# A state-space stage: two tiles per operand, waited for by rotation or by region

## The chip, the cores and the metric

The kernel runs on one core of one Trainium2 chip. The metric is the device time of one execution in microseconds (us). The engines are TensorE (PE, matmuls into the PSUM banks; PEld is its weight loading), VectorE (DVE), ScalarE (ACT), GpSimd (POOL) and SyncE (SP, whose queue issues most of the DMAs). Each engine works through its own instructions in order; between engines, an instruction waits on semaphores.

## The reference

The whole program is a state-space block of two layers with a fusing batch norm, then a sparse quadratic convolution, then two rounds of a Fourier mixing layer and a quantized feed-forward layer, on a batch of 4 images of 96 channels and 64 x 64 points. Only the state-space block matters here. For each of two layers, with 4096 positions, 192 inner channels and 16 states:

```python
h = (seq - mu) * jax.lax.rsqrt(var + EPS) * ln_g + ln_b
xz = h @ in_w
xs, z = jnp.split(xz, 2, axis=-1)
xp = jnp.pad(xs, ((0, 0), (DCONV - 1, 0), (0, 0)))
xc = sum((conv_w[:, k] * xp[:, k:k + L, :] for k in range(DCONV))) + conv_b
xc = jax.nn.silu(xc)
dbl = xc @ xproj_w
...
delta = jax.nn.softplus(dt @ dt_w + dt_b)
dA = jnp.exp(delta[..., None] * A)
dBx = delta[..., None] * Bm[:, :, None, :] * xc[..., None]
hstates = jax.lax.associative_scan(comb, (dA, dBx), axis=1)[1]
y = jnp.einsum('blds,bls->bld', hstates, Cm) + Dp * xc
y = y * jax.nn.silu(z)
return y @ out_w
```

`xc` is the convolution's result and `z` the gate's input of the change's name. In the kernel they are the tiles `xcv` and `zs`.

## The kernel before

The state-space stage is `_mamba`. Its work is cut into 32 **units** (L161 to L164): a unit is one chunk of 512 positions, one layer and one pair of batch images. The 192 inner channels of two images are 384 rows, kept as three parts (k = 0, 1, 2) of 128 partitions: the first 128 channels of each image, and the last 64 of both. `xcv` and `zs` are therefore tiles of 128 x 3 x 512.

A unit has two halves of work. The **front** (`front`, with `norm` before it) makes its operands: six matmul groups `mm_i` (j = 0 to 5, L256 to L267), j = 0 to 2 for the convolution's three parts, with four taps each, j = 3 to 5 for the gate's three parts. ScalarE copies each out of PSUM, into `xcv[:, j, :]` (L275) or `zs[:, k, :]` (L277), then applies SiLU to each whole tile in place (L279, L280). Then come the projection `mm_dbl` from `xcv`, the step sizes `dl`, their product with `xcv` on GpSimd (`du`, L339), and the layouts that are written to DRAM. The **steps** are 24 per unit (three parts, four rows of eight channels, two halves): a DMA broadcasts the step sizes into an `a` tile (L434, eight buffers), ScalarE makes the decays from it (L452), TensorE broadcasts the inputs into a `pq` tile in PSUM (L447, three buffers of two banks), VectorE multiplies it (L457) and scans twice (L469), GpSimd multiplies the scanned states (L475), TensorE sums them into `py` (L488). Every eighth step ends a part: `gate` (L492) on VectorE makes y from `xcv[:, k, :]` and `py` (L496), and GpSimd multiplies it by `zs[:, k, :]` (L497). In a step with `apart` true, GpSimd multiplies a DMA broadcast `db` instead of VectorE a `pq`.

Every `mm_...` tile shares **one** PSUM buffer (tag "mm", one bank), so each matmul group waits until ScalarE or VectorE has read the group before.

The order is written out by hand (`manual_schedule`, L535 on). While the steps of unit n run, the front of unit n+1 is made: generators hand out one piece in each step's `side.slot()`. Within step s the order of issue is: broadcasts of s+2, the sum of an earlier pair of steps, one slot of side work, decays of s+3, the scans of s, the DMAs of later steps, the state copies, and in every eighth step a gate. The gate of part k=0 of a unit is issued in its step 10, that of k=1 in its step 18, that of k=2 in step 2 of the next unit. In that same step 2, in the slot ahead of the gate, the front of the unit after that makes its first write to `xcv`. Two units (the third and the last of the 32) are `late`: their front is issued from step 3 on, behind the output projection of the unit that they need.

`tail` (L359) holds the output projection `mm_o` of the unit before; `norm` normalizes the sequence through `mm_xc`, `mm_v` and `mm_r`, and VectorE writes `hn` from `mm_r` (L249).

The tiles of the change come from `tl(..., bufs=2)`: a rotation of two buffers under one tag. A new tile takes the buffer of the tile two units back, and its first write waits until every instruction that used the old tile is done.

After the stage, `_back` starts with its loads at L699 and uses the same memory; it works on the other layers.

Of the kernel before, what the change touches and what calls it, by code (L numbers as in the profile page):

```python
# [9 lines left out]
F32 = mybir.dt.float32  # L10
# [17 lines left out]
TC = 512  # L28
# [20 lines left out]
def _mamba(ctx, tc, io, w, fd, fstats, xsums):  # L49
# [11 lines left out]
    work = ctx.enter_context(tc.tile_pool(name="mwork", bufs=1))  # L61
# [93 lines left out]
    def col(l, n, k):  # L155

        at = l * 6 + n * 2 + (k == 2)
        return pv[:, at : at + 1]


    units = []  # L161
# [10 lines left out]
    def tag(unit):  # L172
        return "_".join(map(str, unit))

    def mm(nm, unit, shape=None):
        return ps_mm.tile(shape or [128, TC], F32, name=f"mm_{nm}{tag(unit)}", tag="mm")

    def tl(nm, unit, shape, dtype=F32, bufs=1, to=None):
        return work.tile(shape, dtype, name=f"{nm}_{tag(unit)}", tag=to or nm, bufs=bufs)

    def load(unit):
        ch, l, pr = unit
        if l == 0:
            for b in (2 * pr, 2 * pr + 1):
                xt = work.tile([C, TC], F32, name=f"x_{b}_{ch}", tag=f"x{b}")
                nc.sync.dma_start(xt, io["x"][b, :, ch * TC : (ch + 1) * TC])
                seq[b, ch, 0] = xt

    def norm(unit):

        ch, l, pr = unit
        bs = (2 * pr, 2 * pr + 1)
        xc, sqs, ps = {}, {}, {}

        def centred(n):
            xc[n] = tl(f"xc{n}", unit, [C, TC])
            nc.scalar.copy(xc[n], ps[n])
            sqs[n] = tl(f"sq{n}", unit, [C, TC])
            nc.scalar.activation(sqs[n], xc[n], AF.Square)

        for n, b in enumerate(bs):
            ps[n] = mm(f"xc{n}", unit, [C, TC])
            nc.tensor.matmul(ps[n], ctr, seq[b, ch, l], start=True, stop=True)
            if l == 0:
                nc.scalar.activation(
                    tl("xs", unit, [C, TC], to=f"sq{n}"), seq[b, ch, 0], AF.Identity, accum_out=xsums[:, b, ch : ch + 1]
                )
            yield
            centred(n)
            yield "free" if n == 0 else "gap"  # L210
        p_v = mm("v", unit, [128, 8])
        for n in range(2):
            for j in range(4):
                nc.tensor.matmul(
                    p_v[:, n * 4 + j : n * 4 + j + 1], sqs[n][:, j * 128 : (j + 1) * 128], mean1, start=True, stop=True
                )
        yield
        ve = tl("ve", unit, [128, 8])
        r = tl("r", unit, [128, 8])
        vh = tl("vh", unit, [128, 8])  # L220
        a = tl("ra", unit, [128, 8])
        nc.scalar.activation(ve, p_v, AF.Identity, bias=w["eps"])
        nc.scalar.activation(vh, ve, AF.Copy, scale=-0.5)
        yield "gap"
        nc.scalar.activation(r.bitcast(I32), ve.bitcast(I32), AF.Identity, bias=magic, scale=-0.5)
        for _ in range(3):
            nc.gpsimd.tensor_tensor(a, r, r, ALU.mult)
            nc.gpsimd.tensor_tensor(a, a, vh, ALU.mult)
            nc.gpsimd.tensor_scalar(a, a, 1.5, None, ALU.add)
            nc.gpsimd.tensor_tensor(r, r, a, ALU.mult)  # L230
        if ch:
            for b in bs:
                hn = hn_buf[b, l]
                nc.scalar.copy(hn[:, 0:3], hn[:, TC:])
        yield "gap"
        yield "gap"
        for n, b in enumerate(bs):
            p = mm(f"r{n}", unit, [C, TC])
            for j in range(4):
                nc.tensor.matmul(  # L240
                    p[:, j * 128 : (j + 1) * 128],
                    r[:, n * 4 + j : n * 4 + j + 1].to_broadcast([128, C]),
                    ident,
                    start=True,
                    stop=True,
                )
            yield
            yield
            nc.vector.tensor_tensor(hn_buf[b, l][:C, 3:], p, xc[n], ALU.mult)  # L249
            yield "free"  # L250

    def front(unit):
# [3 lines left out]
        for j in range(6):  # L256
            k = j % 3
            p = mm(f"i{j}", unit)
            taps = [(wk[l][:, t, :], t) for t in range(4)] if j < 3 else [(wz[l], 3)]
            for t, (wt, off) in enumerate(taps):  # L260
                cols = slice(off, off + TC)
                f = dict(start=t == 0, stop=t + 1 == len(taps))
                if k < 2:
                    nc.tensor.matmul(p, wt[:, 0:128], hn_buf[bs[k], l][:, cols], **f)  # L264
                else:
                    for n in range(2):
                        nc.tensor.matmul(p[64 * n : 64 * n + 64], wt[:, 128:DIN], hn_buf[bs[n], l][:, cols], **f)  # L267
                if t != 0 and t != 2 or len(taps) == 1:
                    yield
            if j == 0:  # L270
                xcv = tl("xcv", unit, [128, 3, TC], bufs=2)
            if j == 3:
                zs = tl("zs", unit, [128, 3, TC], bufs=2)
            if j < 3:
                nc.scalar.activation(xcv[:, j, :], p, AF.Identity, bias=col(l, 0, k))  # L275
            else:
                nc.scalar.copy(zs[:, k, :], p)  # L277
            yield "free"
# [51 lines left out]
        for at in range(6):  # L330
# [9 lines left out]
            if at >= 3:  # L340

                x, y, t = (t.bitcast(F32) for t in cut[at - 3])
# [192 lines left out]
    with tc.manual_schedule():  # L535
        for n in (0, 1):
            load(units[n])
        side.front = [weights(0), norm(units[0]), front(units[0])]
        side.drain()
        for s in range(5):  # L540
# [7 lines left out]
        for s in range(n_steps + NS):  # L548
# [5 lines left out]
            if at == 0:  # L554
                if n + 1 < len(units) and n + 1 not in late:
                    side.front += ([norm(units[n + 1])] if n == 0 else []) + [front(units[n + 1])]
                    side.norm += [weights(1)] * (n == 0)
            if at == 22 and n + 1 == len(units):
                side.tail.append(way_out(units[n]))
            if at == 3 and 0 < n < len(units):  # L560
                if n + 1 in late:
                    side.front = [tail(units[n - 1]), norm(units[n + 1]), front(units[n + 1])]
                else:
                    side.tail.append(tail(units[n - 1]))
# [5 lines left out]
            if s + 2 < n_steps:  # L570
                unit, k, r, h = steps[s + 2]
# [16 lines left out]
            while live and copied[0] < min(s + 8, n_steps):  # L588
                unit, k, r, h = steps[copied[0]]
# [813 lines left out]
@with_exitstack  # L1403
def kernel(ctx: ExitStack, tc: tile.TileContext, io, out):
    nc = tc.nc
    cp = ctx.enter_context(tc.tile_pool(name="common", bufs=1))
    dp = ctx.enter_context(tc.tile_pool(name="scratch", bufs=1, space=DRAM))
    w = _shared(nc, cp, io)
    p2 = [[dp.tile([2 * C, TC], F32, name=f"p2_{b}_{n}", tag=f"p2_{b}_{n}") for n in range(NCH)] for b in range(B)]
    fd = [dp.tile([C, L], F32, name=f"fd_{b}", tag=f"fd_{b}") for b in range(B)]  # L1410
    with tc.tile_pool(name="stats", bufs=1) as fp:
        fstats = fp.tile([C, B, NCH, 6], F32, name="fstats", tag="fstats")
        xsums = fp.tile([C, B, NCH], F32, name="xsums", tag="xsums")
        with ExitStack() as c:
            _mamba(c, tc, io, w, fd, fstats, xsums)
        with ExitStack() as c:
            _back(c, tc, io, w, fd, fstats, xsums, p2, out)
# [143 lines left out]
```

## Time and profile before

| | |
|---|---|
| median of 3 runs | 5200.37 us (5200.36 to 5221.51) |
| the profiled execution's own time | 5205.16 us |
| its span, first to last instruction | 5203.4 us |
| mean granted TensorE clock | 0.812 |
| busy: PE, DVE, ACT, POOL | 4082.1, 4317.2, 2680.5, 2849.5 us |
| first DMA of `_back` | 3054.44 us |
| DVE busy from 336 to 2861 us | 2331.18 us of 2525 |
| ACT, POOL, PE busy there | 1565.14, 2121.29, 1939.78 us |
| granted clock there | 0.75 |
| DMA share there | 0.85 |

The page gives busy time of each engine over the whole span and in 40 equal slices, each digit the busy share in tenths; a 9 is 90% or more. The row PEclk gives the TensorE clock that was granted, in tenths of full speed. The waits are counted where an engine was idle, and put to the instruction that ended last of those waited for. In an instruction's line of the timeline, "x4" counts the instructions merged into it, and the bracket holds the idle time of its engine just before and what ended it. The stretch from 336 to 2861 us runs from the k=2 gate (L496) of one unit to that of the unit 28 later; these units have a mean period of 90.2 us.

### The profile page before, as it was taken

The numbers are of one execution on the slowest core, as the hardware profiler recorded it, in microseconds if no ns is written. First come the engines' busy times: TensorE is split into PE (matmuls) and PEld (weight loads), VectorE is DVE, ScalarE is ACT, GpSimd is POOL, SyncE is SP. The second block draws the span as 40 slices with busy tenths as digits, with TensorE's granted clock in tenths as the row PEclk, the third lists the DMA queues.
The fourth block names the chain that finished last, engine by engine and source line by source line (L and its number), as shares of the span: only waits on it lengthen the run. The fifth ranks groups of instructions, "written<-read, shape, count | busy, mean of one in ns | idle before, by whom it ended". The sixth has DMA issues, their size and how long they took to land. (4 is left out here: it accounts for less than half of the span.)

```text
span 5203.4 us, 52872 instructions
## 1 busy us (share of the span) xinstructions
PE 4082.1 (78%) x15440; PEld 1752.6 (34%) x15440; DVE 4317.2 (83%) x5639; ACT 2680.5 (52%) x5149; POOL 2849.5 (55%) x2105
## 2 busy tenths in 40 slices
PE   4667877777777778777776728998898898989776
PEld 2222222222222222222222103345455454545565
DVE  2879999999999999999999778979787978787655
ACT  3555665656566665656565410025453444434566
POOL 2768888888888888888888650003130312212122
PEclk7777777777787777777786659999999999999877
DMA  4768888888988888898888754653324333232110
GB/s 111 170 157 207 194 202 206 195 206 194 214 193 201 200 204 206 194 213 191 203 198 207 171 144 142 194 152 94 105 79 145 94 92 111 87 94 81 47 33 21
DMA packets 314048, 800.20 MB, mean 154 GB/s; under 512 B 52247, under 2 KB 58106, under 8 KB 312702
## 3 DMA queue, kind: packets, MB, share of 16 engines
q1 hardware_dynamic: 310174, 790.53, 60.6%
q10 hardware_dynamic: 3584, 6.29, 0.4%
q8 instruction: 123, 2.02, 0.2%
q14 instruction: 167, 1.37, 0.1%
HBM read 703.83 MB, written 67.63 MB: 148 GB/s over the span
## 5 line engine op out<-in xcount | busy, mean ns | idle before, releaser
L475 POOL TENSOR_TENSOR hs<-hs,bc 128x1024 f32<-128x1024 f32 x767 | 1666.4, 2180 | 391.6 <-DVE hs L469 387.1
L469 DVE TENSOR_TENSOR_SCAN hs<-a,hst,pq 128x512 f32<-128x512 f32 x1280 | 1571.4, 1261 | 9.8 <-ACT a L452 9.8
L902 PE MATMUL py<-z,wk 128*96 128x512 f32 x2304 | 1114.8, 613 | 22.1 <-issue 14.3
L457 DVE TENSOR_TENSOR pq<-pq,bc 128x1024 f32<-128x1024 f32 x640 | 775.2, 1211 | 233.3 <-PE pq L447 233.2
L887 DVE TENSOR_TENSOR z<-cp,cp 128x512 f32<-128x512 f32 x1152 | 790.2, 711 | 185.9 <-PE py L902 173.4
L452 ACT ACTIVATE a<-a,aneg 128x512 f32<-128x512 f32 x1280 | 843.9, 711 | 38.4 <-DMA a<-ddl 33.1
L488 PE MATMUL py<-hs,red 128*32 128x512 f32 x3072 | 663.0, 855 | 29.8 <-POOL hs L475 29.5
L902 PEld LDWEIGHTS py<-z,wk 128*96 128x96 f32 x2304 | 366.9, 169 | 446.4 <-issue 315.1
L447 PE MATMUL pq<-uy,sel 64*128 64x512 f32 x768 | 258.2, 637 | 201.4 <-DVE hs L469 200.4
L1152 POOL MEMSET zz<- 96x2 f32 x16 | 1.6, 98 | 745.6 <-ACT zz L1161 651.8
L264 PE MATMUL mm_i<-hn,wk 97*128 97x512 f32 x512 | 322.8, 763 | 106.1 <-ACT xcv L275 80.9
L1253 POOL TENSOR_TENSOR o<-o,fb 128x384 f16<-128x384 f16 x64 | 70.0, 1094 | 546.6 <-ACT o L1258 493.3
L452 ACT ACTIVATE pq<-a,aneg 128x512 f32<-128x512 f32 x256 | 177.0, 692 | 334.0 <-DVE hs L469 322.8
L469 DVE TENSOR_TENSOR_SCAN hs<-pq,hst,db 128x512 f32<-128x512 f32 x256 | 323.7, 1264 | 3.5 <-POOL dx L303 1.5
L275 ACT ACTIVATE xcv<-mm_i,pvec 128x512 f32<-128x512 f32 x96 | 66.0, 687 | 493.4 <-DVE y L496 244.0
L457 POOL TENSOR_TENSOR db<-db,bc 128x1024 f32<-128x1024 f32 x128 | 301.6, 2356 | 14.3 <-DMA db<-ddu 14.3
L447 PE MATMUL pq<-ux,sel 64*128 64x512 f32 x512 | 175.6, 631 | 124.8 <-DMA ux<-ul 65.0
L447 PEld LDWEIGHTS pq<-uy,sel 64*128 64x128 f32 x768 | 98.9, 236 | 477.5 <-DVE hs L469 350.8
L264 PEld LDWEIGHTS mm_i<-hn,wk 97*128 97x128 f32 x512 | 106.8, 232 | 293.0 <-issue 161.0
L1184 PE MATMUL px<-bd,a 128*96 128x128 f32 x1024 | 147.6, 292 | 70.9 <-DVE a L1117 61.6
L1153 POOL TENSOR_TENSOR zz<-zz 96x256 f32<-96x256 f32 x128 | 122.6, 958 | 135.8 <-ACT zz L1160 83.6
L447 PEld LDWEIGHTS pq<-ux,sel 64*128 64x128 f32 x512 | 68.0, 229 | 326.4 <-DVE hs L469 178.8
(286 smaller groups left out, 6532.7 us busy)
## 6 DMA issues: line engine op xcount, KB each, us to landing
a<-ddl SPq DMA_DIRECT2D x768, 512.0 KB, 6.3
cp<-p SPq DMA_DIRECT2D x480, 192.0 KB, 2.7
db<-ddu SPq DMA_DIRECT2D x128, 512.0 KB, 8.3
bc<-ddb SPq DMA_DIRECT2D x64, 512.0 KB, 9.7
cp<-p SPq DMA_DIRECT2D x480, 64.0 KB, 2.7
ddl<-dl SPq DMA_DIRECT2D x128, 192.0 KB, 3.0
tw_k_fwd<-in_k_fwd SPq DMA_DIRECT2D x64, 256.0 KB, 3.3
tw_k_inv<-in_k_inv SPq DMA_DIRECT2D x64, 256.0 KB, 3.0
```

The costliest lines, as they stand in the source:

```text
L264: nc.tensor.matmul(p, wt[:, 0:128], hn_buf[bs[k], l][:, cols], **f)
L447: nc.tensor.matmul(pqs[s][:, i, :], sel[rows, r, :], made[unit][6][k][h][rows], start=True, stop=True)
L452: nc.scalar.activation(to[:, i, :], das[s][:, i, :], AF.Exp, scale=acol(s, i))
L457: engine.tensor_tensor(t, t, bc(unit, 2, k, h), ALU.mult)
L469: nc.vector.tensor_tensor_scan(hss[g][:, at, 1:], d0[:, i, :], d1[:, i, :], hst[pr, l, g % 12][:, at : at + 1], ALU.mult, ALU.add)
L475: (nc.gpsimd if s + 1 < n_steps else nc.vector).tensor_tensor(hs[:, :, :TC], hs[:, :, 1:], bc(unit, 3, k, h), ALU.mult)
L488: nc.tensor.matmul(pys[unit, k][32 * (i // 2 + i % 2 * 2) :][:32], red[:, r, :], hc[:, i, :TC], start=(r == 0), stop=(r == 3))
L887: nc.vector.tensor_tensor(zs[n], cps[q, r0], cps[q, r1], ALU.mult)
L902: nc.tensor.matmul(pys[q], wk[k // KG][:, k % KG, :], zs.pop(n), start=(k == 0), stop=(k == NE - 1))
L1153: nc.gpsimd.tensor_tensor(z0[:, :, 0, :], z0[:, :, 0, :], z1[:, :, 0, :], ALU.add)
L1184: nc.tensor.matmul(p[:, j, :], a2[i % 2][:, kk, :], tabs["bd"][:, int(kk > 0), :], start=True, stop=True)
L1253: nc.gpsimd.tensor_tensor(o2.rearrange("p j c -> p (j c)"), os.pop(g), d["fb2"], ALU.add)
```

## The change

Four tiles are allocated once, ahead of the loops: `xcv0`, `xcv1`, `zs0` and `zs1`, in the same pool, each of the old shape. A unit takes one of each by the parity of its place in the order. No tile is given back within the stage, so there is no release to wait for: each instruction waits for those earlier ones in program order that touched the same region of the tile. The total size is that of the two rotations; the addresses in the pool differ. Every instruction and its place in the order stays.

```diff
@@ -185,6 +185,10 @@
                 xt = work.tile([C, TC], F32, name=f"x_{b}_{ch}", tag=f"x{b}")
                 nc.sync.dma_start(xt, io["x"][b, :, ch * TC : (ch + 1) * TC])
                 seq[b, ch, 0] = xt
+
+    two = {
+        x: [work.tile([128, 3, TC], F32, name=f"{x}{i}", tag=f"{x}{i}", bufs=1) for i in range(2)] for x in ("xcv", "zs")
+    }
 
     def norm(unit):
 
@@ -268,9 +272,9 @@
                 if t != 0 and t != 2 or len(taps) == 1:
                     yield
             if j == 0:
-                xcv = tl("xcv", unit, [128, 3, TC], bufs=2)
+                xcv = two["xcv"][units.index(unit) % 2]
             if j == 3:
-                zs = tl("zs", unit, [128, 3, TC], bufs=2)
+                zs = two["zs"][units.index(unit) % 2]
             if j < 3:
                 nc.scalar.activation(xcv[:, j, :], p, AF.Identity, bias=col(l, 0, k))
             else:
```

## The prediction

> **What bounds the kernel now.** I read first the page's busy times and its 40 slices.
>
> ```profile
> span 5203.4 us, 52872 instructions
> ...
> PE   4667877777777778777776728998898898989776
> DVE  2879999999999999999999778979787978787655
> PEclk7777777777787777777786659999999999999877
> ```
>
> The state-space stage, which the change touches, fills the first 23 slices (to 3055 us, where the first load of the next stage is issued). VectorE is the full engine there: the busy time of the stretch 336 to 2861 us, 28 successive units of (chunk, layer, batch pair), is 2331 us of 2525. Its idle remainder, 194 us, is the most that this stretch can give. TensorE's granted clock is 0.75 on average in the same stretch: it switches between 0.5 and 1.0.
>
> Next the waits of the stage (0 to 2900 us; columns: who waited for whom, us in total, times, longest).
>
> ```profile
> ACT xcv L275 <- DVE y L496: 244.0, 28, 15.2
> ...
> DVE pq L457 <- PE pq L447: 220.9, 132, 49.7
> ...
> PE mm_i L264 <- ACT xcv L275: 89.7, 54, 3.4
> ...
> DVE hn L249 <- PE mm_r L240: 85.5, 47, 13.0
> ```
>
> ScalarE waits for the gate's y (L496) once in each of 28 units, always at the first xcv write. ScalarE is only 52% busy, so the 244 us are no price. A price exists only where the wait reaches VectorE, by TensorE: one PSUM bank serves all mm tiles, so the next mm_i waits for the xcv copy, and the pq broadcasts that VectorE multiplies are queued behind it. So I read one unit in order of time (start, duration, instruction, idle before).
>
> ```profile
> 603.38 1.98 PE L264 MATMUL mm_i<-hn,wk 97*128 97x512 f32 x4
> ...
> 607.64 0.72 DVE L496 SCALAR_TENSOR_TENSOR y<-xcv,pvec,py 128x512 f32<-128x512 f32 x1
> ...
> 608.46 0.69 ACT L275 ACTIVATE xcv<-mm_i,pvec 128x512 f32<-128x512 f32 x1 [8.73 <-DVE y L496]
> ...
> 609.20 3.78 PE L264 MATMUL mm_i<-hn,wk 97*128 97x512 f32 x4 [3.40 <-ACT xcv L275]
> ```
>
> mm_i is complete at 605.36, the copy starts at 608.46: 3.10 us late. TensorE idles 3.40 us and then needs 3.78 us for four matmuls that took 1.98 just before. The stretches of 2 us show why; the last field but two is the granted clock.
>
> ```profile
> 604.00:606.00 2.00, 1.80 (x6) 0.48 (x4) 2.00 (x3) 0.00 (x0) 1.92 (x2) 1.00 1.07 249
> 606.00:608.00 2.00, 0.00 (x0) 0.00 (x0) 2.00 (x3) 0.00 (x0) 0.60 (x2) 0.82 1.02 233
> 608.00:610.00 2.00, 0.80 (x1) 0.50 (x2) 2.00 (x3) 1.54 (x3) 2.00 (x1) 0.50 1.06 242
> ```
>
> The late copy therefore costs twice: the idle itself, and matmuls at half clock for about 10 us behind it. VectorE pays with two stalls.
>
> ```profile
> 613.75 1.23 DVE L457 TENSOR_TENSOR pq<-pq,bc 128x1024 f32<-128x1024 f32 x1 [0.72 <-PE pq L447]
> ...
> 621.65 1.23 DVE L457 TENSOR_TENSOR pq<-pq,bc 128x1024 f32<-128x1024 f32 x1 [1.98 <-PE pq L447]
> ```
>
> **What the wait is.** A rotation of two gives unit n+1 the buffer of unit n-1, and the first write waits for every reader of it. The last reader is the gate of k=2, issued by VectorE in step 2 of unit n; the first xcv write is issued in the same step. By region, xcv[:, 0, :] needs only the readers of part 0: its gate ran 16 steps earlier, some 60 us. Only the third write (part 2) needs the k=2 gate, and starts some 13 us or more behind it. The four units without the wait (the first three and the last) show the new price: the copy starts 0.04 us after mm_i's end.
>
> **Part by part.** No instruction is added, removed or reordered, and no DMA moves.
>
> xcv: over the 28 units the copy is late by 69.5 us in sum (1.0 to 3.1 each, start of the copy less end of mm_i). What of this VectorE pays, I sum from its timeline unit by unit, counting idle over 0.15 us in three parts of the unit after the k=2 gate: front (under 20 us), middle (20 to 60), late (the rest).
> - 12 units with one front stall of 0.42 to 0.44: front 5.1 in sum, middle 2.78 each, late 2.71 each.
> - 3 units without a front stall: middle 2.66, late 2.69. In these the wait was short (TensorE idle 1.55 in the one at 1244 us) and the clock stayed at 1.00.
> - 13 units with 1.31 to 2.76: front 27.1, middle 3.52, late 2.60.
>
> Sum 32.2 + 87.1 + 74.4 = 193.7, the idle found above. The front stalls should go. From below: a unit can't win more than its copy was late if the clock is as before; the smaller of lateness and stall, summed over the units, is 27.2 us. From above: all 32.2. I take 32.2, since the three quiet units had their idle cut to about half, not to none, and stalled not at all; with the wait gone the idle is about the 0.78 us seen before the other mm_i of L267.
>
> Middle: it holds the output projections (L369 to L371) and mm_dbl. In the 13 units it is 3.52 against 2.75 in the other 15, and there the half clock lasts about 10 us around 30 to 40 us after the gate instead of 7. If the front stays at full clock, I expect the 2.75: 13 x 0.77 = 10.0 us. Bounds: 0, and the same 0.77 lost in the other 15 units, -11.6. The late part is alike in all three classes, so I count nothing.
>
> zs: its copies waited for nothing but mm_i (10.0 us in 96 writes), never for POOL's y at L497. 0 us; cover is 15 us of front between that multiply and the first zs write.
>
> Semaphore instructions ahead of L275: 29 of 17 ns before; between none and 96, under 1.7 us either way on an engine with slack. 0.
>
> Placement: the tiles lie elsewhere in SBUF. The nearest rows are the scans, which rotate over buffers and took 1246 to 1273 ns; 12 ns on 1461 scans would be 18 us either way. I take 0, as they show no pattern by buffer.
>
> What is late next: with the front faster, VectorE's next suppliers are POOL (2121 of 2525 us busy, and it waits for VectorE 336 us) and the DMA into a (landing 6.3 us after issue by the page; eight buffers, so some 30 us ahead). VectorE waited for neither in the stretch.
>
> **Sum:** 32.2 + 10.0 = 42 us, 0.8%. On the profiled execution's own 5205.16 us that makes 5163; it lies 4.8 us above the median of the three runs, 5200.37, so I predict **5158**. A measurement of this kernel tells 0.5% (26 us: 5174 and 5226) from no change.
>
> The Trainium skill (TensorE: Matmul & The Clock Gate, section "What's actually happening") has half clock after an idle window of about 3.4 us on a free-running grid. This trace agrees in the grid, the half-clock stretches being multiples of 3.41 us in its clock records, but not in the threshold: the clock fell some 1.8 us after the idle began at 605.8. By that rule only idles of 3.4 would cost clock, and the 32 us would go all the same.
>
> **Rivals.**
> 1. *Given back in the middle.* TensorE, no longer held, reaches its wait for free pq buffers (193.6 us for VectorE's scans in the stretch) sooner, idles there, and meets the projections at half clock in every unit: 32.2 - 11.6 = 20.6 us, 5180. For it: 15 units would have to join the 13. Against: the three quiet units had full clock in front and a middle of only 2.66.
> 2. *Slower: the half clock moves to where nothing covers it.* The same idling, now ahead of the projections and of mm_r, makes each unit as bad as its worst rows: middle 4.15, late 3.77. From 6.92 us of idle a unit (193.7 / 28) it is a loss; at 7.92 it is 28 x 7.92 - 193.7 = +28 us, 5228. For it: the clock in the middle and late parts already falls in every unit. Against: no unit has both maxima. The Trainium skill's page named above, section "A second HAM failure mode: psum-queue depth-cycling", speaks for this one: short idles of a cycling PSUM queue alone make the clock swing. The rows agree so far that the clock swings here with idles under 3.4 us.
> 3. *The wait stays*, because the lasting tile is tracked whole or the copy meets another late reader: 5200. Against: every reader of part 0 is some 60 us old.
>
> **Chances.** Forecast 0.60, own range 5142 (every unit at the 4.86 us of idle of the best one: 28 x 4.86 is 58 under 193.7) to 5173 (27.2 alone). Rival 1: 0.22. Rival 2: 0.10. Rival 3: 0.08. The range 5135 to 5205 takes in rivals 1 and 3 and some placement below 5142; it leaves out rival 2 and a little on the fast side. Faster by over 0.5%: most of the forecast and a quarter of rival 1, 0.62. Slower by over 0.5%: rival 2 at its full price, 0.08. The rest, 0.30.
>
> **What would show it.** Right: the wait of xcv for y gone from the list; the first copy 0.04 us after mm_i; TensorE idle of 0.78 in place of 3.40 ahead of the second mm_i; the clock 1.00 for some 20 us behind the k=2 gate; VectorE idle in the 28 units near 150 us, their mean period near 88.7 instead of 90.2. Wrong: half clock still in the front (rival 2's mechanism), middle stalls of 3.2 in most units (rival 1), or xcv still waiting for y (rival 3). A change of the time after 3055 us would be none of these.

## The result and the profile after

The changed kernel takes **5140.0 us** (median of 4 executions, 5125.2 to 5156.1) against 5202.8 before: ratio 0.9885, 95% interval 0.9853 to 0.9916. It is faster by 1.15%, 63 us; forecast were 42 us and 5158, with an own range of 5142 to 5173, so the measured time lies 2 us beyond its fast edge.

```profile
span 5138.3 us, 52845 instructions
...
DVE  2879999999999999999999877979787978787665
PEclk7676877777877778787877668999999999999876
```

The span is 65.1 us shorter. The first load of the next stage is issued at 2987.2 us instead of 3054.4, so the state-space stage gives 67 us; what follows it takes 2151 us instead of 2149. The 28 units from the second on take 2460.7 us instead of 2524.6. VectorE's idle time in them, in the three parts of a unit that the prediction uses (idle over 0.15 us; profiled executions):

| us in 28 units | front (to 20 us) | middle (20 to 60) | late | sum |
|---|---|---|---|---|
| before | 32.2 | 87.1 | 74.4 | 193.7 |
| after | 5.9 | 62.8 | 64.0 | 132.7 |
| won | 26.3 | 24.3 | 10.4 | 61.0 |

So the front won what was forecast, less 6; the middle won more than twice its 10; the late part, counted at nothing, won 10. Each row is one execution. A second profile of the changed kernel (under the experiments) has 4.7, 52.3 and 63.0: the middle differs by 10 us from one execution to another, the other two parts by 1.

The waits of the changed kernel from 0 to 2900 us, in the columns of before:

```profile
ACT pq L456 <- DVE hs L473: 399.3, 89, 9.6
...
ACT xcv L279 <- PE mm_i L268: 226.2, 39, 16.3
...
DVE pq L461 <- PE pq L451: 174.1, 95, 48.5
...
DVE hn L253 <- PE mm_r L244: 78.6, 48, 13.1
```

The line of xcv waiting for y (244.0 us) is gone; xcv waits for its own matmuls. The first of these lines read so before:

```profile
ACT pq L452 <- DVE hs L469: 295.2, 88, 9.0
```

ScalarE's wait in the decays of an apart step, for VectorE to free a pq buffer, grew from 295.2 to 399.3 us: part of the time that ScalarE had spent waiting for y it now spends there. VectorE's wait for pq fell from 220.9 to 174.1.

One unit of the changed kernel, lines of its timeline (start, duration, instruction, idle before); its k=2 gate starts at 861.6:

```profile
858.79 2.40 PE L268 MATMUL mm_i<-hn,wk 97*128 97x512 f32 x4
861.13 0.49 PE L451 MATMUL pq<-ux,sel 64*128 64x512 f32 x2
861.98 1.98 PE L268 MATMUL mm_i<-hn,wk 97*128 97x512 f32 x4 [0.35 <-ACT xcv L279]
...
865.86 1.42 ACT L456 ACTIVATE pq<-a,aneg 128x512 f32<-128x512 f32 x2 [2.63 <-DVE hs L473]
867.34 0.69 ACT L279 ACTIVATE xcv<-mm_i,pvec 128x512 f32<-128x512 f32 x1
...
878.63 1.42 ACT L456 ACTIVATE pq<-a,aneg 128x512 f32<-128x512 f32 x2 [2.78 <-DVE hs L473]
879.99 0.58 ACT L281 COPY zs<-mm_i 128x512 f32<-128x512 f32 x1
...
880.62 1.97 PE L271 MATMUL mm_i<-hn,wz 97*64 97x512 f32 x4 [2.88 <-ACT zs L281]
...
894.24 1.23 DVE L461 TENSOR_TENSOR pq<-pq,bc 128x1024 f32<-128x1024 f32 x1 [1.00 <-PE pq L451]
```

The second mm_i follows the first with 0.35 us of idle instead of 3.40. The decays at 865.86 wait for VectorE and stand ahead of the second xcv copy, and those of a later apart step (878.63) ahead of a zs copy, so TensorE idles 2.88 us, from 16 to 19 us behind the gate. The stretches (the last field but two is the granted clock) show what follows:

```profile
861.00:864.00 3.00, 2.65 (x9) 0.98 (x8) 3.00 (x4) 2.00 (x4) 2.14 (x1) 1.00 1.06 235
...
876.00:880.00 4.00, 1.74 (x10) 0.30 (x2) 4.00 (x5) 1.33 (x3) 2.82 (x2) 1.00 0.61 146
880.00:884.00 4.00, 3.38 (x10) 0.78 (x14) 4.00 (x4) 3.17 (x7) 4.00 (x3) 0.52 1.00 237
884.00:888.00 4.00, 4.00 (x12) 0.64 (x4) 4.00 (x5) 3.97 (x4) 3.44 (x2) 0.63 1.04 236
888.00:892.00 4.00, 2.99 (x8) 0.92 (x8) 4.00 (x5) 3.88 (x7) 3.40 (x2) 1.00 0.22 50
```

The clock is full through the front, half from 18.5 to 25.4 us behind the gate by the clock records, and full again when the second output projection and mm_dbl run. VectorE stalls once in the middle, 1.00 us, where the units of before lost 2.6 to 4.2. In the unit of before that the prediction reads (gate at 607.6), the clock was half at that place:

```profile
640.00:644.00 4.00, 4.00 (x5) 0.79 (x4) 2.15 (x2) 0.40 (x2) 3.37 (x3) 0.50 0.47 123
```

```profile
645.33 1.23 DVE L457 TENSOR_TENSOR pq<-pq,bc 128x1024 f32<-128x1024 f32 x1 [3.19 <-PE pq L447]
```

Of the 28 units of the changed kernel 16 have no front stall, and 12 of these look like the one shown and are 84.9 to 87.3 us long. In the 12 units with a front stall the clock already falls about 6 us behind the gate and is half for 6.8 us, by the same decays; they lose 0.3 to 0.6 in front and 3.0 on average in the middle. The remaining four are mixed. Two of them (gates at 420.9 and 1830.7) had full clock in front and then lost 5.2 us in the middle, more than any unit of before.

### The profile page after: what moved, and what is told of

Same layout as the page of the kernel before. It is cut to its first block, busy times and chain, and to the rows that moved or that the text cites. A ratio compares the mean times of both kernels' runs of the same rounds, so it can differ in the third digit from the quotient of the medians.

```text
span 5138.3 us, 52845 instructions
## 1 busy us (share of the span) xinstructions
PE 4065.2 (79%) x15440; PEld 1742.3 (34%) x15440; DVE 4317.2 (84%) x5639; ACT 2680.9 (52%) x5149; POOL 2852.7 (56%) x2105
## 5 line engine op out<-in xcount | busy, mean ns | idle before, releaser
L268 PE MATMUL mm_i<-hn,wk 97*128 97x512 f32 x512 | 280.3, 674 | 38.0 <-DVE hn L253 20.8
L279 ACT ACTIVATE xcv<-mm_i,pvec 128x512 f32<-128x512 f32 x96 | 65.5, 683 | 354.7 <-PE mm_i L268 226.2
L271 PE MATMUL mm_i<-hn,wk 97*64 97x512 f32 x512 | 148.5, 711 | 53.7 <-ACT xcv L279 53.7
```

## The experiments

The ratio of each is to the kernel before, run beside it on the same chip. The three numbers are VectorE's idle in the 28 units of its profiled execution, front, middle, late.

**Which of the two operands.** Each alone in two lasting tiles; the other keeps its line with `bufs=2`.

```diff
-        x: [work.tile([128, 3, TC], F32, name=f"{x}{i}", tag=f"{x}{i}", bufs=1) for i in range(2)] for x in ("xcv", "zs")
+        x: [work.tile([128, 3, TC], F32, name=f"{x}{i}", tag=f"{x}{i}", bufs=1) for i in range(2)] for x in ("xcv",)
...
-                zs = two["zs"][units.index(unit) % 2]
+                zs = tl("zs", unit, [128, 3, TC], bufs=2)
```

The second kernel does the same the other way round.

> Only xcv in two lasting tiles, zs back in its rotation of two. Theory (the whole gain comes from the wait of the first xcv copy for the k=2 gate): as the changed kernel, 5125 to 5156 us; no wait of xcv for y, front stalls of VectorE near 6 us in the 28 units instead of 32. Rival (zs or the new places in SBUF matter): 5165 us or more.

> Only zs in two lasting tiles, xcv back in its rotation of two. Theory: as the kernel before, 5195 to 5222 us, with the wait of xcv for y near 244 us. Rival (zs or the new places in SBUF matter): 5180 us or less.

xcv alone: 5136.2 us, ratio 0.9875 (0.9841 to 0.9908); 7.9, 62.0, 66.6. zs alone: 5201.2 us, ratio 0.9992 (0.9969 to 1.0015); 31.3, 89.1, 69.9. The gain is xcv's. The zs tiles, with the new places in SBUF that this kernel has, are worth nothing that can be measured.

**The wait or the clock.** The kernel before, with its wait, but with work that fills the idle: the first two taps of the first mm_i group are run, and then again as the start of the same group.

```diff
+            if j == 0:
+                taps = taps[0:2] + taps
...
-                f = dict(start=t == 0, stop=t + 1 == len(taps))
+                f = dict(start=t == 0 or j == 0 and t == 2, stop=t + 1 == len(taps) or j == 0 and t == 1)
...
-                if t != 0 and t != 2 or len(taps) == 1:
+                if (t in (1, 5) if j == 0 else t != 0 and t != 2 or len(taps) == 1):
```

> The kernel before the change, with the first two taps of the first mm_i group run twice, so that TensorE has 2 us (full clock) of additional matmuls in the idle time in which ScalarE waits for y. The wait itself is kept, and the next mm_i starts no sooner. Theory (the stalls come mostly from the half clock that the idle causes): in the units where the copy was 3.1 us late the front stalls go to 0 to 0.4 us, their sum from 32 to under 18 us, time 5160 to 5195. Rival (the lateness itself costs, or more work costs more): front stalls as before or larger, 5200 us or more.

Measured: 5159.0 us, 1 us under the theory's range, ratio 0.9914 (0.9889 to 0.9938); 11.2, 74.1, 65.3. First a line of its waits, then of its timeline:

```profile
ACT xcv L277 <- DVE y L498: 187.7, 22, 15.2
```

```profile
861.41 3.70 PE L266 MATMUL mm_i<-hn,wk 97*128 97x512 f32 x8
...
867.23 2.58 PE L266 MATMUL mm_i<-hn,wk 97*128 97x512 f32 x4 [1.69 <-ACT xcv L277]
```

The wait for y is still there, 22 times, and the copy still starts behind y. TensorE has two more matmuls in each of 32 units, whose result is overwritten; its idle ahead of the next mm_i is 1.68 us in the median of the 28 units instead of 3.40. That mm_i starts no sooner: 1.55 us behind the gate in the median unit, as in the kernel before. The kernel is 47 us faster for more work (32 to 58 by the interval). Only 3 of 28 units keep a front stall of 1.9 us or more, where 13 had 1.3 or more. So, by this run, most of what the late copy cost was the half clock behind it, not its lateness.

**Filling everywhere.** The changed kernel, every pq broadcast twice.

```diff
-                nc.tensor.matmul(pqs[s][:, i, :], sel[rows, r, :], ...)
+                for _ in range(2):
+                    nc.tensor.matmul(pqs[s][:, i, :], sel[rows, r, :], ...)
```

> The changed kernel with every pq broadcast matmul pair run twice in succession into the same bank, the second overwriting the first with the same values: some 1250 more broadcast matmuls of 0.25 us at full and 0.4 at half clock. Theory (what costs VectorE is the half clock that idle TensorE falls to, more than its work): clock in the stage up from 0.76 to over 0.85, middle and late stalls smaller, time 5100 to 5140. Rival (TensorE's work in line ahead of pq is what costs): 0.5 us more in every step in which VectorE waits for pq, 5170 us or more.

Measured: 5178.5 us, ratio 0.9949 (0.9930 to 0.9969), 38 us slower than the changed kernel; 17.5, 76.5, 81.0. The clock did rise, to 0.81 from 336 to 2700 us against 0.76, but the added matmuls stand in the line that VectorE waits for: its wait for pq from 0 to 2900 us is 203.9 us, against 174.1. The time is the rival's. A higher clock alone does not pay for filler at this place.

**The decays that now hold up the copies.** The changed kernel, with the decays of apart steps behind the slot of side work.

```diff
-                if apart(s + 2):
-                    decays(s + 2)
             if s % 2 == 1 and 2 < s <= n_steps + 1:
                 reduce(s // 2 - 1)
             side.slot()
+            if s + 2 < n_steps and apart(s + 2):
+                decays(s + 2)
```

> The changed kernel, with ScalarE's decays of an apart step, which wait for a free pq buffer, issued behind the step's slot of side work instead of ahead of it. Theory (part of the removed wait went into these decays, 283 to 379 us, and they now hold back the second xcv copy and the second zs copy, so that TensorE idles 2.5 to 2.9 us and falls to half clock): these idles go to 0.4 to 0.8 us, the half clock at 7 to 14 and at 20 to 27 us behind the gate goes, VectorE's idle in the 28 units falls from 133 to 70 to 110 us: 5080 to 5115 us. Rival (the half clock comes from the sum of short idles, whatever the order): within 15 us of the changed kernel, 5125 to 5155.

Measured: 5189.2 us, ratio 0.9970 (0.9952 to 0.9989): a clear miss. No front stall is left (0.0), nor the half clock from 6 us behind the gate on, but the middle went to 146.5 (late 35.0). Stretches, and then lines of VectorE's timeline, of a unit whose gate starts at 1142.7:

```profile
1160.00:1164.00 4.00, 1.36 (x10) 0.34 (x10) 4.00 (x4) 3.95 (x7) 4.00 (x2) 1.00 1.04 248
1164.00:1168.00 4.00, 4.00 (x12) 0.79 (x4) 4.00 (x5) 3.97 (x4) 4.00 (x3) 0.57 1.05 239
1168.00:1172.00 4.00, 4.00 (x6) 1.08 (x6) 3.39 (x4) 2.68 (x5) 3.37 (x3) 0.50 1.01 234
1172.00:1176.00 4.00, 4.00 (x5) 0.79 (x4) 3.06 (x3) 1.13 (x3) 2.64 (x2) 0.50 0.53 129
1176.00:1180.00 4.00, 4.00 (x14) 0.68 (x14) 1.94 (x2) 0.58 (x1) 2.43 (x2) 0.50 0.51 139
1180.00:1184.00 4.00, 3.31 (x10) 0.54 (x8) 2.82 (x3) 1.16 (x2) 2.18 (x1) 0.80 0.00 0
```

```profile
1178.06 1.23 DVE L461 TENSOR_TENSOR pq<-pq,bc 128x1024 f32<-128x1024 f32 x1 [3.01 <-PE pq L451]
1186.80 1.28 DVE L473 TENSOR_TENSOR_SCAN hs<-pq,hst,db 128x512 f32<-128x512 f32 x1 [3.98 <-POOL dx L307]
```

Two things happened. TensorE, faster in front, ran into its wait for VectorE's scan just ahead of the projections (1.36 us busy of 4 from 1160), the clock fell, and it stayed at half for some 17 us in which TensorE was busy throughout. That is the mechanism of the prediction's second rival; 16 of the 28 units have the same stall of 3.01 us. And the scan at 1186.80 waited 3.98 us for decays that now stood behind ScalarE's other work (the releaser that the profile names, POOL, had long been done).

The same move in the two steps where it helps, and then with fillers:

```diff
-                if apart(s + 2):
+                if apart(s + 2) and at not in (4, 8):
                     decays(s + 2)
...
             side.slot()
+            if s + 2 < n_steps and apart(s + 2) and at in (4, 8):
+                decays(s + 2)
```

> As the kernel with the decays behind the slot, but only in steps 4 and 8 of a unit, where the side work is the second xcv and the second zs copy. Theory (that order took the front stalls away, and what it lost were decays that came to stand behind long ScalarE work in steps 9 to 13, VectorE's scan stalls of 1.4 to 4.1 us at 37 to 45 us behind the gate, near 80 us in sum): no front stalls, no scan stalls, 5095 to 5130 us. Rival (the half clock in the middle of the unit costs what the front gains, since TensorE now waits 2.6 us for VectorE right ahead of the projections): 5135 us or more, with middle stalls of 3.0 us and more in over half the units.

Measured: 5147.8 us (5119.0 to 5154.9), ratio 0.9875 (0.9841 to 0.9909); 0.0, 73.0, 55.6. The scan stalls and front stalls are gone, and the time is that of the changed kernel: in 13 of 28 units VectorE loses 3.0 us at the projections and 4.6 to 6.0 in the whole middle, in the others at most 0.24. The time is the rival's. That the middle took just what the front gave is not shown, since two executions of the changed kernel differ as much in the middle (62.8 and 52.3).

**Fillers ahead of the projections.** On that kernel, the gate's last matmul group (j = 5, 1.1 us) is computed twice, the second result over the first; further, or instead, the first output projection (3.2 us).

```diff
+            if j == 5:
+                taps = taps * 2
...
-                f = dict(start=t == 0, stop=t + 1 == len(taps))
+                f = dict(start=t == 0 or j == 5, stop=t + 1 == len(taps) or j == 5)
```

```diff
+            for _ in range(2 - n):
                 nc.tensor.matmul(p, ow[:, 0, :], ys[unit, n], start=True, stop=False)
...
```

> The kernel before this one in the list, with the gate's last matmul group (j = 5) computed twice into the same bank, the second result overwriting the first: 1.1 us more of TensorE work at full clock just ahead of its wait for VectorE's scan. Theory (idle there drops the clock, and the projections then run at half clock): the clock stays at 1.00 up to some 40 us behind the gate in most units, middle stalls under 1 us, 15 to 50 us faster than without the filler. Rival (the added work is just more work): same time or up to 30 us slower, the middle stalls as without it.

> The kernel with decays behind the slot in steps 4 and 8, with two fillers: the gate's last matmul group (j = 5) twice, and the first output projection of a unit (three matmuls, 3.2 us at full clock) twice into the same bank. The second filler lies where TensorE waits some 2.7 us for ScalarE's copy in units whose clock is full. Theory (with the idle filled, the half clock at 20 to 40 us goes in most units): middle stalls under 1 us in at least 20 of the 28 units, 5090 to 5120 us. Rival (where the clock is half at 22 us, the filler costs 3 to 6 us more, and the units in that state stay in it): 5150 us or more.

> As the kernel with two fillers, without the first (only the first output projection twice). Theory: as that kernel or up to 20 us slower, since the wait ahead of the projections still drops the clock. Rival (the added matmuls run mostly at half clock): 5160 us or more.

> The changed kernel itself beside the two others on the same chip, to have its spread: 5120 to 5160 us in each execution, the profile with units of two kinds, near 85 and near 90 us long, in another mixture than in the first profile.

The last group twice: 5161.6 us, ratio 0.9896 (0.9851 to 0.9940); 0.0, 86.7, 62.7, the rival's time and not the theory's. In 15 units the clock is full past the first idle and falls at the next one, where TensorE waits for ScalarE's copy of the first projection; in 8 it still falls at the first. Both fillers: 5131.9 us, ratio 0.9869 (0.9834 to 0.9905); 0.0, 50.7, 65.5, between theory and rival: the middle is under 1 us in 16 units, not in 20. The projection alone: **5248.7 us**, ratio 1.0092 (1.0063 to 1.0121); 0.0, 173.8, 67.9, the rival's time. The last two differ by 1.1 us of matmuls whose result is thrown away in each unit, and the kernel that has them is 117 us faster. Without them the projections run at half clock in 15 of the 28 units, and doubling one then costs, as this unit's VectorE shows:

```profile
644.57 0.75 DVE L501 SCALAR_TENSOR_TENSOR y<-xcv,pvec,py 128x512 f32<-128x512 f32 x1 [4.49 <-PE mm_o L374]
649.20 1.23 DVE L462 TENSOR_TENSOR pq<-pq,bc 128x1024 f32<-128x1024 f32 x1 [2.69 <-PE pq L452]
655.79 1.23 DVE L462 TENSOR_TENSOR pq<-pq,bc 128x1024 f32<-128x1024 f32 x1 [3.01 <-PE pq L452]
```

The changed kernel again: 5136.0 us, ratio 0.9875 (0.9843 to 0.9907). 4.7, 52.3, 63.0. 19 of its 28 units have no front stall (16 in the first profile): the mixture changes from one execution to another, and the time with it (5127.1 and 5140.0 us in the two profiled executions).

**A better version.** Both fillers in the regular units alone, and the last group twice (`taps * 2`) or three times (as shown).

```diff
-            if j == 5:
-                taps = taps * 2
+            if j == 5 and 2 < units.index(unit) < 31:
+                taps = taps * 3
...
-                if t != 0 and t != 2 or len(taps) == 1:
+                if (t + 1 == len(taps) if j > 2 else t in (1, 3)):
...
-            for _ in range(2 - n):
+            for _ in range(2 if n == 0 < units.index(unit) < 29 else 1):
```

> The kernel with two fillers, in the regular units alone: the last gate group twice in the 28 units from the fourth on, the first projection twice in the 28 tails that are not issued ahead of a late front. Theory: the stretch of 28 units as with the fillers everywhere (2443 us), the last two units at 104 and 78 us as in the changed kernel instead of 108 and 84: 5110 to 5130 us. Rival (the mixture of units shifts to the slow kind in other executions): 5135 us or more.

> As the kernel with fillers in the regular units, with the last gate group computed three times, 2.2 us of filler in a wait of 2.6. Theory (the half clock at 22 to 25 us of half the units comes from the 1.8 us of idle that one filler leaves): it goes in most units, the gate's wait for py of 1.3 us with it, 5090 to 5120 us. Rival (the filler delays the pq broadcast, which was to be issued in that wait): 5130 us or more.

Twice: 5137.5 us (5103.3 to 5140.9), ratio 0.9869 (0.9840 to 0.9898); 0.0, 39.1, 64.2 in its fastest execution, the profiled one: the rival's time. Three times: **5068.4 us** (5062.3 to 5083.3), ratio 0.9749 (0.9723 to 0.9775), faster than forecast and some 70 us under the changed kernel; 0.0, 17.0, 59.8. Stretches of a unit whose gate starts at 857.1:

```profile
876.00:880.00 4.00, 3.08 (x16) 0.59 (x12) 4.00 (x5) 3.97 (x6) 4.00 (x3) 1.00 0.66 166
880.00:884.00 4.00, 4.00 (x10) 1.09 (x9) 4.00 (x5) 3.97 (x5) 3.39 (x3) 1.00 1.04 234
884.00:888.00 4.00, 3.76 (x10) 1.09 (x10) 3.64 (x4) 2.06 (x5) 2.92 (x2) 1.00 0.48 108
888.00:892.00 4.00, 4.00 (x20) 0.77 (x19) 3.75 (x4) 1.86 (x3) 3.97 (x2) 1.00 0.58 135
```

The clock stays at 1.00 from the gate to 40 us behind it or later, in all 28 units, and every unit's idle in the middle is 0.6 us.

## Why the prediction was right

*The bound and the chain.* Right: the wait reached VectorE by TensorE, and no work was added or removed. xcv alone carries the gain. The 52% given for ScalarE is its share of the whole span; in the stretch it is 62% (1565 of 2525 us), which leaves the argument as it is.

*The front, 32.2 us.* Right in mechanism, 26.3 in size. The copy starts 0.04 us behind mm_i as said, and the idle ahead of the second mm_i is 0.35 us. I took that idle as the only one left, and the clock as full for 20 us: 16 of 28 units have no front stall, and in 15 of these the clock is full for 18 to 19 us. In the other 12 ScalarE's decays, waiting for a pq buffer, hold the second xcv copy. I named POOL and the DMA as the next late ones and not these decays, although their wait stood in the list of before with 295 us. In the kernels that move the decays, the front stalls are 0.0.

*The middle, 10.0 us.* The mis-sized term: 24.3. I took the 2.75 us of the quieter units of before as the price of a middle with a good front. All of those still had half clock near 30 to 37 us, at the projections. The 12 quiet units after have the half clock earlier, at 18 to 26 us, and full clock from there to 42 us, when the second projection and mm_dbl run; they lose 0.8 to 1.1. It can be lower yet: 0.6 with the last group three times. For the same reason the fast edge of the forecast's range was no bound: it gave every unit the 4.86 us of idle of the best unit of before, and these 12 units have 2.2 to 3.7.

*The late part, 0.* Measured 10.4, in the 16 units without a front stall (2.03 each; 2.7 in a unit of before). Not separated by an experiment. That the total came within 20 us is in part luck: what the front fell short by covers some of what the middle and the late part won beyond the sum.

*zs, semaphores and placement, 0.* The zs kernel, 0.9992, confirms zs and its own placement to some 0.3%; the scans that the placement term leans on took 1243 to 1285 ns, a little wider than quoted. The semaphores ahead of the xcv copy were not tried alone.

*The double cost, idle and half clock.* The kernel with the wait kept and its idle filled gives 47 of the 63 us, so by this run the clock is the larger part. It wins 13 us in the middle too; that this part would carry so far into the middle is what the sum missed. One reading was off: the clock records have half clock from 607.26 us, 1.5 us after the idle began at 605.8, and not 1.8.

*Rivals.* The first (given back in the middle) did not come in the sum, but two of the 28 units show it with 5.2 us each, and 13 units of the kernel with the decays moved in steps 4 and 8 show it with 4.6 to 6.0. The second (half clock moved to the projections) did not come either; the kernel with the decays behind the slot shows its mechanism, with 3.0 us at the projections in over half its units, but not its price, since it is still no slower than the kernel before. The third fell: no wait for y is left.

The rule cited from the Trainium skill (TensorE: Matmul & The Clock Gate, "What's actually happening"), half clock after an idle window of some 3.4 us and full clock after a busy one, held for the sign, not for its amounts: here the clock fell with idles of 1.79 us (the kernel with the last group twice, 618.94), 2.64 us (decays behind the slot, 1163.26) and 2.88 us (the changed kernel, 880.62), and 17 us of busy time did not end half clock.

## What to carry to other kernels

A wait on an engine that is far from full can still set the pace, if the engine that it stops falls to half clock; look in the rows behind a wait for the granted clock and for durations that double, and count both. When such a wait is removed, list all waits of the same engine that stood close behind it: they come next, and the part of the loop after them may take the gain or add to it. Where TensorE has to wait in any case, matmuls that recompute a result just ahead of the wait can be worth more than they cost, and a little too little, or at another place, does harm; each needs its own run.

## What the runs showed of the hardware

- TensorE at half clock and busy without a break (4.00 of 4.00 us in three stretches) stayed at half clock for some 17 us, through the output projections (1164 to 1181 us of the kernel with the decays behind the slot). What ends this state was not found; whether it is the shape of these matmuls was not tried.
- From 336 to 2700 us all changes of the clock lie on one grid of 3.41 us, to within 5 ns, in each of the 14 traces. In the traces before and after, the busy share of TensorE in each stretch of this grid was set beside the clock of the next stretch. The 92 and 90 falls came behind stretches that were at most 0.74 busy, in the median 0.46 and 0.42; the clock stayed full behind stretches of at least 0.57 and 0.53, in the median 0.80 and 0.85. A dividing line at 0.57 puts all but 20 of 354 and 22 of 364 on the right side. The clock rose only behind stretches that were at least 0.86 busy, but 77 and 70 stretches that were over 0.99 busy did not raise it. So a fall goes with the idle that one stretch of the grid holds: with 2.64 us in one piece the clock fell (decays behind the slot, 1163.26), with 0.92 us ahead of the projections (last group three times, 877.58) it did not.
- Two kernels that differ by 1.1 us of repeated matmuls a unit are 117 us apart (5131.9 and 5248.7), and executions of one kernel spread over 31 us (5125 to 5156), with the units' two kinds in other mixtures. The place of a unit's gate on that grid goes with its kind: in the changed kernel 15 of the 16 units without a front stall have it 1.4 to 2.4 us behind a grid line, and the other 12 have it between 3.1 us and, past the next line, 1.2 us. In the second profile of this kernel it is 17 of 19, at 1.3 to 2.8 us, and the other 9 lie at 0 to 1.4 us. No run moved the grid, so this is read from the traces and not tested.
